# One core, sixteen batches: the last batch's final layer norm rearranged, and the planner's ranks changed

## The chip, the core and the metric

The kernel runs on one core of a Trainium2 chip. The metric is the device time of one execution in microseconds (us). Engines are named as in the profile: PE is TensorE's matmul, PEld its weight load, DVE is VectorE, ACT ScalarE, POOL GpSimd, SP SyncE, which here only issues DMA transfers (SPq in the profile).

## The reference, cut to what matters

The input x has 16 batches of 1024 nodes by 128 features; adj is a symmetric 1024x1024 matrix of zeros and ones. Two layers follow each other, each with a residual and a layer norm without weights:

```python
x = _layernorm(x + gnn_0(x, adj, ...), axis=-1)      # graph attention
x = _layernorm(x + gnn_1(x, adj, adj, ..., 5), axis=-1)  # gated, 5 steps
```

Layer 0 computes attention over pairs of nodes, masked by adj, as one product of adj with scaled features. Layer 1 repeats this step five times for every batch, with h of 1024x128 as state (in_matrix and out_matrix are both adj, and the biases are zero):

```python
m = einsum('nm,bmd->bnd', adj, h)          # messages; av = [m, m]
u3 = h @ u3_w.T + u3_b
z = sigmoid(av @ w3_w.T + w3_b + u3)
r = sigmoid(av @ w4_w.T + w4_b + u3)
hv = tanh(av @ w5_w.T + w5_b + (r * h @ u5_w.T + u5_b))
h = (1.0 - z) * h + z * hv
```

and ends, for every batch, with `layernorm(y + h)`, where y is what layer 0 gave (the "layer input" below). All values are fp32.

## The kernel before, in words

State is held transposed: hT of a batch is 128 features by 1024 nodes, worked in two halves of 512 columns, e = 0 and 1. Batches go in pairs q (batches 2q and 2q+1). For most pairs the messages of both batches are made together, with seven products in place of eight (sums of quarters, "tab"), from copies of h that are turned on VectorE and through DRAM (T, away to X, back to G). For the first pair's first three steps and the last pair's last three steps (`PLAIN`) each batch has its own messages (tiles ps_acc and blk_h).

Per batch, step and half, `gates` issues: the product with u3 (pu, L1103), ScalarE's copy of it into the bank of z (L1106), the products for r and z on top (L1113), their tanh (L1116, a sigmoid by halves), r times h on VectorE (L1123), the two products for the candidate (pv, L1129 and L1130), its tanh (hv, L1133), and three VectorE operations that make the new h: subtract (L1140), times (L1147), add (L1154).

`leave` is what follows a step. After the last one, for each half g: h is transposed back (on PE for the last three batches, L523, as `on_pe` says), the layer input is loaded again from DRAM (yd) into a tile o (L1197), VectorE adds the two (L1205), `layernorm` runs, and o goes out (L1216). `layernorm` has four parts: statistics on VectorE (four bn_stats L492, four bn_aggr L494), on GpSimd the power -1/2 of the variance and a bias from the mean (L498 to L505), and on ScalarE four operations of 128x128 that scale and shift (L510). Even batches carry the negative of h, so sign(b) is -1 for them and +1 for odd ones. The tiles o have two buffers; y0, layer 0's own result tile, has two as well and is not used once layer 0 is done.

The order in which every engine gets its instructions is not the order of the code. `Plan.add` records each operation with its engine, a length, a rank and what it reads and writes; `Plan.order` then plays the program through: an engine that is free takes, of the operations that are ready, the one with the lowest rank. Lengths on VectorE and ScalarE are taken 15% longer (`MARGIN`), and a fixed lag is added between engines. The hardware engines then run their lists strictly in that order, each waiting for what its next instruction needs. So a rank changes the order of lists and nothing else.

A step of a batch has the rank `10*(b//2) + 4.2*s`, and its operations are set off from it by the table `D` (m is the copy of messages, pu, pr, pz, pv the products, u, r, z, hv the ScalarE and VectorE work on them, h the three last operations, tr the turn or transposition, o the residual add and the load of the layer input, ln the layer norm, out the output). `LATER` is added for batch 15 in its last three steps, so that batches 14 and 15 take turns. Layer 0 and the look at adj have ranks of their own.

`IDLE` is the number of pairs of transposes of the identity that PE is given with rank 9000, that is, whenever the plan has nothing else ready for it. Each pair has a planned length of 2x109 ns. All write to one tile, ("ps", "idle"), which takes one of six "ps" banks from the first to the last of them.

Of the kernel before, what the change touches and what calls it, by code (L numbers as in the profile page):

```python
# [18 lines left out]
HALF = 512  # L19
# [6 lines left out]
LOW, HIGH = -20.0, 100.0  # L26
TINY = 1e-30
PLAIN = {(0, 0), (0, 1), (0, 2), (7, 2), (7, 3), (7, 4)}
LATER = 3
TURNED = {(7, 3)}  # L30
IDLE = 100


class Plan:
# [98 lines left out]
def kernel(  # L133
# [79 lines left out]
    def exact(pools):  # L213
# [62 lines left out]
        def chunks(ap):  # L276

            return ap.rearrange("p (b c i) -> p c b i", b=4, c=4)
# [5 lines left out]
        def pe(*a, **k):  # L284
            plan.add("PE", *a, **k)

        def dve(*a, **k):
            plan.add("DVE", *a, **k)

        def act(*a, **k):  # L290
            plan.add("ACT", *a, **k)
# [2 lines left out]
            plan.add("SP", *a, **k)  # L294


        D = dict(m=-0.4, pu=1.4, u=0.4, pr=0.8, pz=1.4, r=-0.3, pv=0.2, z=0.3, hv=0.2, h=0.6, tr=1.0, o=3.6, ln=3.9)
        D.update(out=4.2, l1=-9, l2=-5, l3=-4, l4=-4, l5=-5, l6=-3.5, l7=-1, l8=0)

        def on_pe(b, what):  # L300

            return b < 2 and what in ("y", "b") or b >= B - 3 and what == STEPS - 1 or (b // 2, what) in TURNED
# [181 lines left out]
            dve(2 * V, 1 + c / 4, t24, reads=[*y, (("tab",), c, 0)], writes=[(("tab",), c, 1)])  # L484


        def layernorm(key, g, rank, after, src, dst, write, sg=1):
            stats, mv, rstd = ("stats", *key, g), ("mv", *key, g), ("rstd", *key, g)

            def look():  # L490
                for j in range(4):
                    nc.vector.bn_stats(T(stats)[:, j, :], src(j))  # L492
                for j in range(4):
                    nc.vector.bn_aggr(T(mv)[:, j, :], T(stats)[:, j, :])  # L494

            def power():
                mean, var, r = T(mv)[:, :, 0], T(mv)[:, :, 1], T(rstd)
                nc.gpsimd.tensor_scalar(r[:, 0, :], var, EPS, None, ALU.add)  # L498
                nc.gpsimd.tensor_tensor(r[:, 0, :], r[:, 0, :], mhalf[:, 0:4], ALU.pow)
                if sg > 0:  # L500
                    nc.gpsimd.tensor_scalar(r[:, 1, :], mean, -1.0, None, ALU.mult)
                    nc.gpsimd.tensor_tensor(r[:, 1, :], r[:, 1, :], r[:, 0, :], ALU.mult)
                else:
                    nc.gpsimd.tensor_tensor(r[:, 1, :], mean, r[:, 0, :], ALU.mult)
                    nc.gpsimd.tensor_scalar(r[:, 0, :], r[:, 0, :], -1.0, None, ALU.mult)  # L505

            def scale():
                r = T(rstd)
                for j in range(4):
                    nc.scalar.activation(  # L510
                        dst(j), src(j), AF.Identity, bias=r[:, 1, j : j + 1], scale=r[:, 0, j : j + 1]
                    )

            dve(1100, rank, look, reads=[after], writes=[(stats, 0), (mv, 0)])
            plan.add("POOL", 2200, rank, power, reads=[(mv, 0)], writes=[(rstd, 0)])
            act(1250, rank, scale, reads=[after, (mv, 0), (rstd, 0)], writes=[write])

        def transposes(src, read, t, rank):


            def emit():
                for j in range(4):
                    nc.tensor.transpose(T(t)[:, j * P : (j + 1) * P], src()[:, j * P : (j + 1) * P], ident)  # L523

            pe(4 * TR, rank, emit, reads=[*read, (("ident",), 0)], writes=[(t, 0)])

        def turn(t, src, read, rank):

# [436 lines left out]
        def messages(q, s, k):  # L965
# [118 lines left out]
            combine(m[one, 1], c, ALU.add)  # L1084
            return [[(m[one, 0], 0), (m[one, 1], "part")], [(m[two, 1], "part")] * 2]

        def gates(b, s, soon):
            rank = rank_of(b, s)
            hT = ("hT", b)
            sg = sign(b)  # L1090


            for e in range(2):
                m, r, z, hv = (k + (b, s, e) for k in (("m",), ("r",), ("z",), ("hv",)))
                pr, pz, pv = ("ps", "g", b, s, e, "r"), ("gz", b, s, e), ("ps", "g", b, s, e, "v")
                mark = (("after",), b, s, e)

                def h(e=e):
                    return T(hT)[:, hs[e]]


                def pu_(pr=pr, h=h):
                    nc.tensor.matmul(T(pr), u3, h(), start=True, stop=True)  # L1103

                def u_(pr=pr, pz=pz):
                    nc.scalar.copy(T(pz), T(pr))  # L1106

                pe(F, rank + D["pu"], pu_, reads=[(hT, e), (("uw",), 0), soon[b % 2][e]], writes=[(pr, 0), mark])
                act(A, rank + D["u"], u_, reads=[(pr, 0)], writes=[(pz, 0)])
                for p_, t, j, due in ((pr, r, 1, "r"), (pz, z, 0, "z")):  # L1110

                    def gate_(p_=p_, j=j, m=m):
                        nc.tensor.matmul(T(p_), wm[:, j, :], T(m), start=False, stop=True, skip_group_check=True)  # L1113

                    def sig_(p_=p_, t=t, j=j):
                        nc.scalar.activation(T(t), T(p_), AF.Tanh, bias=bh[:, j : j + 1], scale=0.5 * sg)  # L1116

                    pe(F, rank + D["p" + due], gate_, reads=[(m, 0), mark, (pz, 0), (("wm",), 0)], writes=[(p_, 1)])
                    act(A, rank + D[due], sig_, reads=[(p_, 1)], writes=[(t, 1)])
                dve(  # L1120
                    V,
                    rank + D["r"],
                    lambda r=r, h=h: nc.vector.scalar_tensor_tensor(T(r), T(r), 1.0, h(), ALU.add, ALU.mult),  # L1123
                    reads=[(r, 1), (hT, e)],
                    writes=[(r, 2)],
                )

                def pv_(pv=pv, m=m, r=r):
                    nc.tensor.matmul(T(pv), wm[:, 2, :], T(m), start=True, stop=False)  # L1129
                    nc.tensor.matmul(T(pv), u5h, T(r), start=False, stop=True)  # L1130

                def hv_(pv=pv, hv=hv):
                    nc.scalar.activation(T(hv), T(pv), AF.Tanh, bias=b5 if sg > 0 else nb5, scale=1.0)  # L1133

                pe(2 * F, rank + D["pv"], pv_, reads=[(m, 0), (r, 2), (("wm",), 0), (("uw",), 0)], writes=[(pv, 0)])
                act(A, rank + D["hv"], hv_, reads=[(pv, 0), (("wm",), 0)], writes=[(hv, 0)])
                dve(
                    V,
                    rank + D["h"],
                    lambda hv=hv, h=h: nc.vector.tensor_tensor(T(hv), T(hv), h(), ALU.subtract),  # L1140
                    reads=[(hv, 0), (hT, e)],
                    writes=[(hv, 1)],
                )
                dve(
                    V,
                    rank + D["h"],
                    lambda hv=hv, z=z: nc.vector.scalar_tensor_tensor(T(hv), T(z), 1.0, T(hv), ALU.add, ALU.mult),  # L1147
                    reads=[(hv, 1), (z, 1)],
                    writes=[(hv, 2)],
                )  # L1150
                dve(
                    V,
                    rank + D["h"],
                    lambda hv=hv, h=h: nc.vector.scalar_tensor_tensor(h(), T(hv), 0.5, h(), ALU.mult, ALU.add),  # L1154
                    reads=[(hv, 2)],
                    writes=[(hT, e)],
                )

        def leave(b, s):

# [2 lines left out]
            for g in range(2):  # L1163
# [18 lines left out]
                    continue  # L1182

                t = ("ps", "t", b, s, g)
                if on_pe(b, s):
                    transposes(h, [(hT, g)], t, rank + D["tr"])
                else:
                    t = ("F", b, s, g)
                    turn(k, h, [(hT, g)], rank + D["tr"])
                    away(k, d, rank + D["tr"])  # L1190
                    back(d, t, rank + D["o"])

                o, yd = ("o", b, g), ("yd", b, g)
                sp(
                    450,
                    rank + D["o"],
                    lambda o=o, yd=yd: nc.sync.dma_start(T(o).rearrange("p c d -> p (c d)"), T(yd)),  # L1197
                    reads=[(yd, 0), (hT, g)],
                    writes=[(o, "y")],
                )  # L1200

                def last(t=t, o=o, flat=on_pe(b, s)):
                    x = T(o).rearrange("p c (a j) -> p c a j", a=4)
                    n = T(t).rearrange("p (c a j) -> p c a j", c=4, a=4) if flat else chunks(T(t))
                    nc.vector.tensor_tensor(x, n, x, ALU.add)  # L1205

                dve(V, rank + D["o"], last, reads=[(t, 0), (o, "y")], writes=[(o, "raw")])

                def at(j, o=o):
                    return T(o)[:, j, :]  # L1210

                layernorm(("o", b), g, rank + D["ln"], (o, "raw"), at, at, (o, 0), sign(b))
                sp(
                    450,
                    rank + D["out"],
# [343 lines left out]
```

## Time and profile before

| | us |
|---|---|
| runs of the kernel before, median of 3 (lowest, highest) | 1466.42 (1464.65, 1471.49) |
| the profiled execution: its own time | 1466.58 |
| its span, from the first to the last instruction | 1464.7 |
| PE busy / DVE busy / ACT busy / POOL busy in the span | 1442.1 / 1168.4 / 898.9 / 152.9 |
| idle transposes (L413): count, first and last start | 200, 4.9 and 49.4 |
| last product of the gates (L1130): start | 1447.99 |
| last scaling (L510): end | 1460.49 |

A row of a timeline gives the start, the length, the engine, the line and the operation with its output and inputs; "x4" means that four of them were merged into one row, and the bracket tells how long the engine was idle before it and what ended that. In a row of waits the figures are the total in us, how often, and the longest. [...] what counts for PE's rate is the distance between starts, 0.43 us for the fp32 products of the gates and 0.233 us for those with the messages' rounded type.

### The profile page before, as it was taken

How to read it: one execution, taken by the hardware profiler on the slowest of the kernel's cores; microseconds unless marked ns; L12 is line 12 of the kernel's file. 1: busy time of each engine (PE TensorE's matmuls, PEld its weight loads, DVE VectorE, ACT ScalarE, POOL GpSimd, SP SyncE). 2: the span in 40 equal slices, each digit the busy share in tenths (PEclk: the TensorE clock that was granted, in tenths of full speed). 3: DMA queues.
4: the chain of work that ended last, by engine and by line, in shares of the span. 5: the costliest groups of instructions: out<-in, count | busy, mean ns of one | idle time of the engine just before them, and what ended most of it. 6: DMA issues, size and time to landing. Idle time of an engine off the chain costs nothing.

```text
span 1464.7 us, 17943 instructions
## 1 busy us (share of the span) xinstructions
PE 1442.1 (98%) x5052; PEld 904.6 (62%) x5052; DVE 1168.4 (80%) x2757; ACT 898.9 (61%) x1792; POOL 152.9 (10%) x265
## 2 busy tenths in 40 slices
PE   9999899999999999999999999999999999999995
PEld 7766665666666666665566656665666665665563
DVE  6887788888888788888888888887888877757444
ACT  5456565676657666576756676566674666555544
POOL 0201000011002020110201120011110202000102
PEclk9999999999999999999999999999999999999998
DMA  4145534654335542464433643355433464223301
GB/s 164 58 126 162 167 78 117 172 177 128 87 100 151 173 131 65 121 172 140 117 98 117 187 123 94 108 161 155 116 85 96 134 184 114 58 72 87 91 24 45
DMA packets 208384, 174.21 MB, mean 119 GB/s; under 512 B 34879, under 2 KB 158486, under 8 KB 208278
## 3 DMA queue, kind: packets, MB, share of 16 engines
q1 hardware_dynamic: 207714, 172.15, 41.1%
q10 hardware_dynamic: 564, 0.85, 0.2%
q8 instruction: 41, 0.67, 0.2%
q14 instruction: 65, 0.53, 0.1%
HBM read 94.63 MB, written 78.29 MB: 118 GB/s over the span
## 4 chain that ended last, share of the span: by engine, by line
PE 94%; DVE 2%; DMA 1%; ACT 1%; POOL 1%; issue 0%; SPq 0%; POOLq 0%; DVEq 0%
PE ps_acc_a L573 17%; PE ps_g_r L1113 9%; PE ps_g_v L1129 9%; PE ps_g_v L1130 9%; PE gz L1113 9%; PE ps_g_r L1103 9%; PE ps_acc_c L573 8%; PE ps_acc_po L573 8%; PE ps_acc L573 6%; PE gz L573 4%; PE ps_g_ph L602 2%; PE ps_idle L413 1%; PE ps_acc_po L872 1%; PE ps_acc_px L858 1%; ACT o L510 1%; DMA blk_boot<-in_adj_dram 0%
## 5 line engine op out<-in xcount | busy, mean ns | idle before, releaser
L1129 PE MATMUL ps_g_v<-m,wm 128*128 128x512 f32 x320 | 163.4, 592 | 0.0
L1130 PE MATMUL ps_g_v<-r,u5h 128*128 128x512 f32 x320 | 163.3, 592 | 0.0
L1140 DVE TENSOR_TENSOR hv<-hv,hT 128x512 f32<-128x512 f32 x160 | 109.7, 687 | 63.2 <-ACT hv L1133 62.8
L1113 PE MATMUL ps_g_r<-m,wm 128*128 128x512 f32 x320 | 158.8, 594 | 1.1 <-ACT gz L1106 1.1
L1113 PE MATMUL gz<-m,wm 128*128 128x512 f32 x320 | 157.7, 592 | 0.0
L1103 PE MATMUL ps_g_r<-hT,u 128*128 128x512 f32 x320 | 152.7, 592 | 0.0
L1123 DVE SCALAR_TENSOR_TENSOR r<-r,hT 128x512 f32<-128x512 f32 x160 | 109.1, 686 | 50.9 <-ACT r L1116 50.1
L573 PE MATMUL ps_acc_a<-tab,blk_s 128*128 128x512 f32 x544 | 146.7, 411 | 0.4 <-ACT m L1056 0.4
L573 PE MATMUL ps_acc_po<-adj,blk 128*128 128x512 f32 x512 | 144.5, 428 | 0.0
L1116 ACT ACTIVATE r<-ps_g_r,bh 128x512 f32<-128x512 f32 x160 | 109.4, 686 | 46.8 <-PE ps_g_r L1113 46.5
L573 PEld LDWEIGHTS ps_acc_a<-tab,blk_s 128*128 128x128 f32 x544 | 100.4, 188 | 34.4 <-issue 6.7
L1116 ACT ACTIVATE z<-gz,bh 128x512 f32<-128x512 f32 x160 | 109.5, 688 | 19.1 <-PE gz L1113 18.8
L573 PEld LDWEIGHTS ps_acc_po<-adj,blk 128*128 128x128 f32 x512 | 96.0, 188 | 39.4 <-issue 14.6
L1154 DVE SCALAR_TENSOR_TENSOR hT<-hv,hT 128x512 f32<-128x512 f32 x160 | 107.9, 676 | 1.6
L1147 DVE SCALAR_TENSOR_TENSOR hv<-z,hv 128x512 f32<-128x512 f32 x160 | 108.1, 677 | 1.0 <-ACT z L1116 0.3
L1106 ACT COPY gz<-ps_g_r 128x512 f32<-128x512 f32 x160 | 91.5, 574 | 28.1 <-PE ps_g_r L1103 26.7
L531 DVE STREAM_TRANSPOSE T<-hT 128x512 f32<-128x512 f32 x150 | 104.9, 701 | 4.1 <-DMA X<-T 3.7
L1130 PEld LDWEIGHTS ps_g_v<-r,u5h 128*128 128x128 f32 x320 | 60.5, 189 | 76.8 <-issue 61.9
L1113 PEld LDWEIGHTS gz<-m,wm 128*128 128x128 f32 x320 | 60.5, 190 | 74.4 <-issue 74.0
L573 PE MATMUL ps_acc<-adj,blk_h 128*128 128x512 f32 x384 | 99.9, 416 | 3.9 <-DVE blk_h L565 3.9
L1133 ACT ACTIVATE hv<-ps_g_v,nb 128x512 f32<-128x512 f32 x80 | 54.9, 689 | 68.6 <-PE ps_g_v L1130 68.6
L1113 PEld LDWEIGHTS ps_g_r<-m,wm 128*128 128x128 f32 x320 | 59.4, 189 | 58.5 <-issue 44.6
(166 smaller groups left out, 2520.7 us busy)
## 6 DMA issues: line engine op xcount, KB each, us to landing
G<-X SPq DMA_DIRECT2D x152, 256.0 KB
X<-T SPq DMA_DIRECT2D x600, 64.0 KB
yd<-y SPq DMA_DIRECT2D x32, 256.0 KB
o<-yd SPq DMA_DIRECT2D x32, 256.0 KB
out_dram<-o SPq DMA_DIRECT2D x32, 256.0 KB
xt<-in_x_dram SPq DMA_DIRECT2D x15, 512.0 KB
pb<-ud SPq DMA_DIRECT2D x14, 512.0 KB
D_y<-T_y SPq DMA_DIRECT2D x112, 64.0 KB
```

Source lines behind the costliest of these rows:

```text
L531: nc.vector.transpose(T(t).rearrange("p (b c i) -> p b c i", b=4, c=4), turned(src()))
L573: nc.tensor.matmul(T(bank), T(blk)[:, k, c, :], right(c), start=(first and i == 0), stop=(last and i == len(terms) - 1), skip_group_check= ...
L1103: nc.tensor.matmul(T(pr), u3, h(), start=True, stop=True)
L1106: nc.scalar.copy(T(pz), T(pr))
L1113: nc.tensor.matmul(T(p_), wm[:, j, :], T(m), start=False, stop=True, skip_group_check=True)
L1116: nc.scalar.activation(T(t), T(p_), AF.Tanh, bias=bh[:, j : j + 1], scale=0.5 * sg)
L1123: lambda r=r, h=h: nc.vector.scalar_tensor_tensor(T(r), T(r), 1.0, h(), ALU.add, ALU.mult),
L1129: nc.tensor.matmul(T(pv), wm[:, 2, :], T(m), start=True, stop=False)
L1130: nc.tensor.matmul(T(pv), u5h, T(r), start=False, stop=True)
L1140: lambda hv=hv, h=h: nc.vector.tensor_tensor(T(hv), T(hv), h(), ALU.subtract),
L1147: lambda hv=hv, z=z: nc.vector.scalar_tensor_tensor(T(hv), T(z), 1.0, T(hv), ALU.add, ALU.mult),
L1154: lambda hv=hv, h=h: nc.vector.scalar_tensor_tensor(h(), T(hv), 0.5, h(), ALU.mult, ALU.add),
```

## The change

It does seven things.

1. The layer input of batch 15 is loaded into tiles of the kind y0 (keyed `("y0", b, "o", g)`), not o, and the load has the rank of the step itself, not +3.6; it waits for the first m of that step, not for h. For all batches the planned lag of this load is now 2300 ns.
2. `layernorm` gets a form `short`: GpSimd makes only the power (and its negative for even batches), and VectorE scales with four `tensor_scalar` operations, (x - mean) times r. It is used for both halves of batch 15 and for the second half of batch 14.
3. `pieces` is 2 for batch 15 in its last step: hv, the three operations on h, the transposes and the residual add are made in pieces of 256 columns.
4. `LATER` goes from 3 to 2.
5. `IDLE` goes from 100 to 140.
6. In `D`, for all batches: pz from 1.4 to 1.2, z from 0.3 to 0.5, tr from 1.0 to 1.2, out from 4.2 to 4.0.
7. Some planned lengths follow from this (a half tanh 400, a half VectorE operation V/2+40, the short scaling 900, GpSimd 1700).

```diff
-LATER = 3
+LATER = 2
-IDLE = 100
+IDLE = 140
...
-        D = dict(m=-0.4, pu=1.4, u=0.4, pr=0.8, pz=1.4, r=-0.3, pv=0.2, z=0.3, hv=0.2, h=0.6, tr=1.0, o=3.6, ln=3.9)
-        D.update(out=4.2, l1=-9, l2=-5, l3=-4, l4=-4, l5=-5, l6=-3.5, l7=-1, l8=0)
+        D = dict(m=-0.4, pu=1.4, u=0.4, pr=0.8, pz=1.2, r=-0.3, pv=0.2, z=0.5, hv=0.2, h=0.6, tr=1.2, o=3.6, ln=3.9)
+        D.update(out=4.0, l1=-9, l2=-5, l3=-4, l4=-4, l5=-5, l6=-3.5, l7=-1, l8=0)
...
-                if sg > 0:
+                if short:
+                    if sg < 0:
+                        nc.gpsimd.tensor_scalar(r[:, 0, :], r[:, 0, :], -1.0, None, ALU.mult)
+                elif sg > 0:
...
+            def scale_short():
+                for j in range(4):
+                    nc.vector.tensor_scalar(
+                        dst(j), src(j), T(mv)[:, j, 0:1], T(rstd)[:, 0, j : j + 1], ALU.subtract, ALU.mult
+                    )
+            if short:
+                dve(900, rank, scale_short, reads=[*after, (mv, 0), (rstd, 0)], writes=[write])
+            else:
+                act(1250, rank, scale, reads=[*after, (mv, 0), (rstd, 0)], writes=[write])
...
+        def pieces(b, s):
+            return 2 if b == B - 1 and s == STEPS - 1 else 1
...
+                n = pieces(b, s)
+                for i in range(n):
+                    w = slice(i * HALF // n, (i + 1) * HALF // n)
...
+                    length = V if n == 1 else V / n + 40
+                    act(A if n == 1 else 400, rank + D["hv"], hv_, reads=[(pv, 0), (("wm",), 0)], writes=[(hv, 0, i)])
+                    dve(length, rank + D["h"], less_, reads=[(hv, 0, i), (hT, e)], writes=[(hv, 1, i)])
+                    dve(length, rank + D["h"], times_, reads=[(hv, 1, i), (z, 1)], writes=[(hv, 2, i)])
+                    dve(length, rank + D["h"], h_, reads=[(hv, 2, i)], writes=[(hT, e) if n == 1 else (hT, e, i)])
...
-                o, yd = ("o", b, g), ("yd", b, g)
+                o, yd = ("y0" if b == B - 1 else "o", b, "o", g), ("yd", b, g)
                 sp(
                     450,
-                    rank + D["o"],
+                    rank + (D["o"] if b < B - 1 else 0),
                     lambda o=o, yd=yd: nc.sync.dma_start(T(o).rearrange("p c d -> p (c d)"), T(yd)),
-                    reads=[(yd, 0), (hT, g)],
+                    reads=[(yd, 0), (hT, g) if b < B - 1 else (("m", b, s, 0), 0)],
                     writes=[(o, "y")],
+                    lag=2300,
                 )
+                for i in range(n):
...
+                    dve(V / n, rank + D["o"], last, reads=[(t, i), (o, "y")], writes=[(o, "raw", i)])
...
                     sign(b),
+                    b == B - 1 or b == B - 2 and g,
                 )
```

## The prediction

> **What bounds the kernel now.** I read the page's busy shares first, then TensorE's own waits, then busy time by stretch, then the end in order of time. Page, part 1:
>
> ```profile
> PE 1442.1 (98%) x5052; PEld 904.6 (62%) x5052; DVE 1168.4 (80%) x2757; ACT 898.9 (61%) x1792; POOL 152.9 (10%) x265
> ```
>
> TensorE (PE) has work for 98% of the span. The view of waits, for PE alone, lists nearly all of its waiting:
>
> ```profile
> PE ps_acc L573 <- DVE blk_h L565: 3.9, 1, 3.9
> PE ps_t L523 <- DVE hT L1154: 2.8, 2, 2.4
> PE gz_fill L417 <- POOL ones L383: 1.3, 1, 1.3
> PE ps_g_r L1113 <- ACT gz L1106: 1.1, 2, 0.7
> PE ps_p L679 <- DVE T_ws L398: 1.0, 1, 1.0
> ```
>
> So a rank can win only three things: the one long wait (first line), small waits of under 1 us, and the end, where PE is done early. Busy time by stretch, around the long wait and at the end (columns: stretch, length, busy us of PE, weight load, VectorE, ScalarE, GpSimd, then PE's granted clock, DMA share, GB/s):
>
> ```profile
> 149.00:153.20 4.20, 0.35 (x2) 0.03 (x1) 4.17 (x7) 2.03 (x6) 0.00 (x0) 0.92 0.82 235
> 153.20:159.50 6.30, 6.27 (x15) 4.94 (x16) 2.72 (x12) 1.22 (x3) 0.00 (x0) 0.51 0.69 193
> 159.50:165.00 5.50, 5.50 (x25) 4.03 (x24) 1.57 (x3) 3.41 (x6) 0.00 (x0) 1.00 1.01 351
> ```
>
> PE stands from 149 to 153.2 while VectorE is full (4.17 of 4.20), and then runs 6.3 us at a clock of 0.51. The stall costs 3.9 us plus about 3.1 us (6.3 x 0.49) of slow clock: 7.0 us. The end, in order of time (start, length, engine, line, operation, idle before):
>
> ```profile
> 1442.06 7.48 SPq L1216 DMA_DIRECT2D out_dram<-o  x2
> ...
> 1443.16 1.13 PE L1113 MATMUL ps_g_r<-m,wm 128*128 128x512 f32 x2 [0.41 <-ACT gz L1106]
> ...
> 1446.04 0.69 ACT L1133 ACTIVATE hv<-ps_g_v,b 128x512 f32<-128x512 f32 x1 [1.03 <-PE ps_g_v L1130]
> ...
> 1447.49 1.64 ACT L510 ACTIVATE o<-o,rstd_o 128x128 f32<-128x128 f32 x4
> ...
> 1449.03 0.67 ACT L1133 ACTIVATE hv<-ps_g_v,b 128x512 f32<-128x512 f32 x1
> 1449.59 2.32 SPq L1197 DMA_DIRECT2D o<-yd  x2
> ...
> 1452.53 0.69 DVE L1205 TENSOR_TENSOR o<-ps_t,o 128x512 f32<-128x512 f32 x1 [0.59 <-DMA o<-yd]
> ...
> 1458.84 1.65 ACT L510 ACTIVATE o<-o,rstd_o 128x128 f32<-128x128 f32 x4 [0.37 <-POOL rstd_o L502]
> ```
>
> The reload of the layer input (L1197) leaves SP only at 1449.59, because the output of batch 14 (L1216) stands before it in SP's order, waiting for ScalarE's scaling to end. VectorE's first residual add (L1205) waits for that load until 1452.53. One scaling (L510 at 1447.49) stands before the last tanh (L1133, 1449.03). From the end of the last scaling (1460.49) to the end of the span are 4.2 us of output transfer.
>
> [...] 4 us of idle, then 0.51 for 6.3 us. [...] here the stretch from 22.6 to 28.5 us holds, but for eight tiny products at its end, only 50 idle transposes and keeps a clock of 1.00, so the trace decides: idle transposes keep the clock. [...]
>
> **The change, part by part: the end.** All of this lies after the last PE work and is on the path.
>
> Reload: it moves from rank +3.6 to the start of step 4 of batch 15 (trigger: the first m) and goes to y0 tiles, which layer 0 has left long ago. That m is copied at about 1433, so it lands before it is needed, and one DMA issue (0.4 us) goes ahead of batch 14's outputs on SP, which do not start before 1442.06: free. What is late next is VectorE itself.
>
> Pieces: the last step of batch 15 has 8 chain instructions (2 tanh, 6 VectorE) and 2 residual adds, which become 16 and 4. At full size VectorE starts one every 0.605 us (L475/L476 rows near 53 us); [...] The six halves of an e take 2.04 us against 1.81: more work, but the first starts after a tanh of 0.47 instead of 0.69.
>
> Scaling: four 128x128 operations on VectorE instead of four of 480 ns on ScalarE (1.65 us in all). The nearest row is L433, a 128x128 tensor_scalar of 216 ns; with the spacing of the bn_stats (four in 0.87 us) as the upper end, 0.6 to 0.87; I take 0.66. GpSimd's two last operations (0.24 + 0.20 us, 0.6 with their gaps) go for batch 15. For the second half of batch 14 the scaling leaves ScalarE, and with it what stood before the last tanh; its 0.66 us is now on VectorE, behind batch 15's lower ranks.
>
> LATER 3 to 2: batch 15 moves one rank forward. Its u3 products of step 3 have rank 84.6+1.4 = 86.0, now below batch 14's messages of step 4 (86.8); before it was 87.0. So the two batches' gates are done in turn instead of mixed, and batch 14's first scaling (L510 at 1440.38, which held up the gz copy) comes earlier. A batch alone in its gates costs no wait in the trace: from 1388.28 to 1396.58 batch 14 alone does its 20 matmuls of 0.43 us (8.6) without a gap. I count the 0.57 us lost before 1443.16 as gone.
>
> The sum: first tanh 1446.04-0.57 = 1445.47; +0.47+0.05: VectorE starts at 1445.99; six halves: 1448.03. The last product starts 0.57 earlier, 1447.42, and its tanh 0.63 later as for the first e (1445.41 to 1446.04), 1448.05; +0.52: 1448.57; six halves: 1450.61; four half adds (1.36): 1451.97; two sets of statistics at 1.15 (1453.25 to 1454.40): 1454.27; to GpSimd 0.45 and its two operations 1.35: 1456.07; scaling 0.1+0.66: 1456.83; output 4.2: 1461.0. Against 1464.7 that is 3.7 us. If the 0.57 stays and batch 14's scaling comes between, it is 2.5; if the first e's adds and statistics fit in VectorE's gaps, up to 5.
>
> **The rest of the program.** D's new ranks hold for all batches: z products before u3 products, z's tanh after the u copy, the turn of h (and so its away and back transfers on SP) after the combining of messages, outputs earlier on SP. Behind a later turn stand its four DMA issues (1.8 us on SP) and the fetch of G; ScalarE already waits 31.7 us for G without PE standing. Since PE has no wait of note between 165 and 1440, nothing is to be gained there beyond about 1 us; the loss is bounded by one more stall of the size above, 7.0. I take 0.
>
> IDLE 100 to 140 adds 80 transposes at 0.109 us: 8.7 us of PE work. In the trace the 100 pairs are used up at 49.5, so the new ones go to later places where the planner sees PE idle. Laid into the long wait they cost nothing and keep the clock: -3.1. Laid where PE is really full they cost 0.218 a pair, +8.7 at most. The wait takes 18 pairs; that leaves 22, part of which will fall in the planner's gaps between 50 and 149 that the trace does not show as waits. I take 14 of them uncovered (+3.1) against the clock (-3.1): 0, with both ends kept.
>
> Forecast: 3.7 us less. The profiled execution took 1466.58 with 1464.7 of span (1.9 around it); the median is 1466.42, so the step is the same there: **1462.7 us**.
>
> **Rivals.**
> First, the long wait itself goes: VectorE's queue there (six h operations, two turns, then blk_h) is ordered anew, or idle work keeps the clock and some of the wait falls away. For it: it hangs on the order of one queue. Against: blk_h has rank 8.4 and all that stands ahead (4.8 to 8.0) stays ahead under the new ranks. 1462.7-7.0 to 1462.7-3.1: about 1457.
> Second, slower: the idle pairs are uncovered. The planner counts VectorE and ScalarE 15% long, so it sees gaps on PE that are none; each pair there pushes all later work. It decides from 17 pairs on (3.7/0.218). All 40: 1462.7+8.7 = 1471.4.
> Third: the shared idle tile keeps one of six ps banks until its last use, 49.5 us before and perhaps far later now, or a later turn makes PE wait for messages: one or two stalls of 7.0, 1469.7 to 1476.7.
>
> **How the numbers follow.** Forecast 0.43, first rival 0.22, second 0.18, third 0.17. What can be told from no change is about 0.5%, 7.3 us: under 1459.1 and over 1473.7. The first rival lies nearly whole under it, with a little of the forecast's spread: 0.23; the third by more than half, the second partly: 0.19; 0.58 between. The likeliest case alone reaches from 1460 to 1466; for 8 in 10 the range goes from 1456 to 1474.
>
> **What would show it.** In the changed profile: o<-yd issued before batch 14's outputs; no wait of L1205 for a DMA; L1133 and the three h lines at 128x256 near 340 ns apart; PE's last product near 1447.4 plus what came before; from there 13.6 us to the end instead of 16.7. The idle tile's last use and PE's clock after 149 us show which idle case holds. I am wrong if PE shows a new wait of over 2 us in the middle, or idle matmuls between products that had no gap before.

## The result and the profile after

| | before | after |
|---|---|---|
| median of the runs (lowest, highest), us | 1468.95 (1464.65, 1471.49), 7 runs | 1479.81 (1476.23, 1482.15), 7 runs |
| ratio after/before, 95% interval | | 1.0079 (1.0064 to 1.0093) |
| span of the profiled execution | 1464.7 | 1479.9 |
| start of the last product of the gates | 1447.99 | 1465.05 |
| from there to the end of the span | 16.71 | 14.82 |

The kernel became 0.8% slower. 1462.7 had been forecast with a range to 1474, so the result lies outside on the slow side. In the later series of runs the kernel before took 1465.35 to 1466.73 us (medians), not 1468.95; against 1466 the kernel after would stand at 1.0094, and that is the value to set beside the ratios of the experiments. The last two rows divide it: the end, which nearly the whole prediction was about, became 1.9 us shorter. All that comes before it, which the prediction put at nothing, became 17.1 us longer.

In what follows lines are numbered as in the kernel after. L1120, L1123, L1130, L1133, L1140, L1147 and L1155 are the gates' L1103, L1106, L1113, L1116, L1123, L1130 and L1133 of before; L586 is L573 (messages), L574 and L578 are L561 and L565 (a block for the messages is cut into two parts), L513 is L510 (scaling on ScalarE), L519 the new scaling on VectorE. Kernels made from the one before keep its numbers.

Busy time on the page of the kernel after:

```profile
PE 1452.9 (98%) x5132; PEld 912.3 (62%) x5132; DVE 1169.6 (79%) x2777; ACT 892.8 (60%) x1782; POOL 147.2 (10%) x260
```

PE still has work for 98% of the span. It is busy for 10.8 us more, and 8.7 of these are the 80 new idle transposes at 0.109 us. What PE waited for (total us, how often, longest):

```profile
PE ps_g_r L1130 <- ACT gz L1123: 6.3, 5, 2.1
PE ps_t L536 <- DVE hT L1164: 2.4, 1, 2.4
PE ps_acc L586 <- DVE blk_h L578: 2.3, 3, 1.6
PE ps_g_v L1147 <- DVE r L1140: 1.8, 1, 1.8
PE gz_fill L417 <- POOL ones L383: 1.3, 1, 1.3
```

Where one wait of 3.9 us headed this list before, five waits for ScalarE's copy gz do now. Busy time by stretch around the old long wait, same columns as before:

```profile
149.00:153.20 4.20, 3.72 (x15) 2.42 (x14) 3.07 (x7) 2.44 (x6) 2.64 (x4) 1.00 0.20 53
153.20:159.50 6.30, 6.30 (x31) 4.61 (x30) 6.09 (x15) 4.70 (x12) 0.00 (x0) 1.00 0.74 237
```

All but 0.48 us of the long wait is gone, and PE's clock stays at 1.00. So 6.5 of the 7.0 us were won there, and the loss elsewhere must be more than 17. The idle transposes did not do it. One tile's instructions, the idle tile's (shortest, median and longest ns, first and last start):

```profile
L413 PE MATMUL ps_idle<-ident x280: 271/273/476, 4.9 to 1388.0; 128*128 128x128 f32 x140
```

All but 66 are used up by 51 us; these stand in twelve small groups between products from 194 to 1388 us, 18 of them at 829.5, and none in the old long wait.

What the new waits look like shows at the longest one. The timeline of the kernel after, columns as before:

```profile
877.63 2.74 PE L1120 MATMUL ps_g_r<-hT,u 128*128 128x512 f32 x6
...
878.20 3.59 POOL L507 TENSOR_TENSOR rstd_o<-mv_o,rstd_o 128x4 f32<-128x4 f32 x1
...
881.87 0.24 POOL L508 TENSOR_SCALAR rstd_o<-rstd_o 128x4 f32<-128x4 f32 x1
882.15 1.65 ACT L513 ACTIVATE o_o<-o_o,rstd_o 128x128 f32<-128x128 f32 x4 [3.63 <-POOL rstd_o L508]
...
883.70 1.05 ACT L1123 COPY gz<-ps_g_r 128x512 f32<-128x512 f32 x2
...
884.33 3.55 PE L1130 MATMUL ps_g_r<-m,wm 128*128 128x512 f32 x4 [2.10 <-ACT gz L1123]
```

From the bottom up: PE stood 2.10 us for gz (ScalarE's copy of the u3 product). ScalarE could have copied it as soon as the u3 product was there (L1120, from 877.63), but its list has a layer norm's scaling first (L513), and that stood 3.63 us for GpSimd, whose operation L507 took 3.59 us. The plan counts 2200 ns for all of GpSimd's part; here it took over 5. The scaling has no hurry; but ScalarE's list is run in order, and the copies behind the scaling start at 883.70, as it ends, and are late with it.

The wait costs PE more than its length. Busy time by stretch just behind it:

```profile
884.60:888.00 3.40, 3.40 (x5) 1.36 (x5) 0.69 (x1) 1.48 (x4) 0.20 (x2) 0.50 0.49 119
```

For 3.4 us the clock is at 0.50, which is 1.7 us more. In the kernel before, half clock came with the wait of 3.9 us (0.50 from 152.5 to 159.3 us); here it came behind one of 2.10 us. What makes it come isn't shown: behind the wait of 2.37 us that ends at 1451.99 us in the kernel before, PE's four transposes (0.66 us) still ran at 1.00.

The wait at 860.8 us (1.80, the page's "DVE r") is of the same kind on VectorE. The chain of waits of the kernel after (start, length, what):

```profile
853.85 4.41 DMA F<-X
...
858.29 0.70 DVE o_o L1231
...
861.95 0.61 DVE r L1140
...
862.60 1.13 PE ps_g_v L1147 x2
```

A residual add (L1231) waits for a fetch of 4.41 us that is planned at 2.3, and r, for which PE waits, comes behind it on VectorE.

Last, the end:

```profile
1464.62 1.02 PE L1147 MATMUL ps_g_v<-r,u5h 128*128 128x512 f32 x2
...
1465.66 1.11 DVE L519 TENSOR_SCALAR o_o<-o_o,mv_o,rstd_o 128x128 f32<-128x128 f32 x4
1465.68 0.84 ACT L1155 ACTIVATE hv<-ps_g_v,b 128x256 f32<-128x256 f32 x2 [1.03 <-PE ps_g_v L1147]
1466.68 0.76 DVE L1158 TENSOR_TENSOR hv<-hv,hT 128x256 f32<-128x256 f32 x2
...
1468.60 1.09 PE L536 MATMUL ps_t<-ident,hT 128*128 128x128 f32 x4 [2.36 <-DVE hT L1164]
...
1469.72 0.76 DVE L1231 TENSOR_TENSOR y_o<-ps_t,y_o 128x256 f32<-128x256 f32 x2 [0.27 <-PE ps_t L536]
...
1474.42 1.12 DVE L519 TENSOR_SCALAR y_o<-y_o,mv_o,rstd_o 128x128 f32<-128x128 f32 x4 [0.22 <-POOL rstd_o L499]
```

No residual add of batch 15 waits for a DMA any more, and the pieces are there. But the scaling of batch 14's second half (L519, 1.11 us) stands on VectorE right where the last pieces could start.

### The profile page after: what moved, and what is told of

It is laid out like the page before. It is cut to its first block, busy times and chain, and to the rows that moved or that the text cites. A ratio compares the mean times of both kernels' runs of the same rounds, so it can differ in the third digit from the quotient of the medians.

```text
span 1479.9 us, 18030 instructions
## 1 busy us (share of the span) xinstructions
PE 1452.9 (98%) x5132; PEld 912.3 (62%) x5132; DVE 1169.6 (79%) x2777; ACT 892.8 (60%) x1782; POOL 147.2 (10%) x260
## 4 chain that ended last, share of the span: by engine, by line
PE 86%; DMA 4%; DVE 3%; SPq 2%; ACT 2%; issue 1%; POOL 1%; DVEq 0%; POOLq 0%; ACTq 0%
PE ps_acc_a L586 15%; PE ps_g_r L1130 8%; PE ps_g_v L1147 8%; PE ps_g_v L1146 8%; PE ps_g_r L1120 8%; PE gz L1130 8%; PE ps_acc_po L586 8%; PE ps_acc_c L586 8%; PE ps_acc L586 5%; PE gz L586 4%; DMA G<-X 2%; SPq L554 2%; PE ps_idle L413 2%; PE ps_g_ph L615 2%; PE ps_acc_po L885 1%
## 5 line engine op out<-in xcount | busy, mean ns | idle before, releaser
L1130 PE MATMUL ps_g_r<-m,wm 128*128 128x512 f32 x320 | 161.0, 601 | 7.5 <-ACT gz L1123 6.3
L1147 PE MATMUL ps_g_v<-r,u5h 128*128 128x512 f32 x320 | 163.4, 592 | 1.8 <-DVE r L1140 1.8
L1158 DVE TENSOR_TENSOR hv<-hv,hT 128x512 f32<-128x512 f32 (+1 forms) x162 | 110.2, 682 | 65.4 <-ACT hv L1155 65.2
L1130 PE MATMUL gz<-m,wm 128*128 128x512 f32 x320 | 158.5, 593 | 0.0
L1140 DVE SCALAR_TENSOR_TENSOR r<-r,hT 128x512 f32<-128x512 f32 x160 | 109.6, 689 | 60.1 <-ACT r L1133 59.3
L1120 PE MATMUL ps_g_r<-hT,u 128*128 128x512 f32 x320 | 153.8, 592 | 0.0
L586 PE MATMUL ps_acc_a<-tab,blk_s 128*128 128x512 f32 x544 | 148.4, 414 | 0.8 <-ACT m L1069 0.8
L586 PE MATMUL ps_acc_po<-adj,blk 128*128 128x512 f32 x512 | 142.8, 425 | 0.0
L1133 ACT ACTIVATE r<-ps_g_r,bh 128x512 f32<-128x512 f32 x160 | 109.5, 686 | 53.1 <-PE ps_g_r L1130 52.8
L586 PEld LDWEIGHTS ps_acc_a<-tab,blk_s 128*128 128x128 f32 x544 | 100.8, 188 | 33.5 <-issue 9.6
L586 PEld LDWEIGHTS ps_acc_po<-adj,blk 128*128 128x128 f32 x512 | 96.0, 188 | 37.9 <-issue 12.5
L1133 ACT ACTIVATE z<-gz,bh 128x512 f32<-128x512 f32 x160 | 109.7, 688 | 14.9 <-PE gz L1130 14.3
L1123 ACT COPY gz<-ps_g_r 128x512 f32<-128x512 f32 x160 | 91.3, 572 | 37.6 <-PE ps_g_r L1120 36.3
L1164 DVE SCALAR_TENSOR_TENSOR hT<-hv,hT 128x512 f32<-128x512 f32 (+1 forms) x162 | 108.6, 673 | 1.2
L1147 PEld LDWEIGHTS ps_g_v<-r,u5h 128*128 128x128 f32 x320 | 60.4, 189 | 79.0 <-issue 62.6
L1161 DVE SCALAR_TENSOR_TENSOR hv<-z,hv 128x512 f32<-128x512 f32 (+1 forms) x162 | 108.4, 671 | 0.8 <-ACT z L1133 0.2
L1130 PEld LDWEIGHTS gz<-m,wm 128*128 128x128 f32 x320 | 60.6, 191 | 74.6 <-issue 74.3
L586 PE MATMUL ps_acc<-adj,blk_h 128*128 128x512 f32 x384 | 101.6, 414 | 2.3 <-DVE blk_h L578 2.3
L1130 PEld LDWEIGHTS ps_g_r<-m,wm 128*128 128x128 f32 x320 | 59.3, 190 | 63.3 <-issue 39.3
L1155 ACT ACTIVATE hv<-ps_g_v,nb 128x512 f32<-128x512 f32 x80 | 54.9, 688 | 68.8 <-PE ps_g_v L1147 68.5
```

What stands on the lines that cost most here:

```text
L586: nc.tensor.matmul(T(bank), T(blk)[:, k, c, :], right(c), start=(first and i == 0), stop=(last and i == len(terms) - 1), skip_group_check= ...
L1158: nc.vector.tensor_tensor(T(hv)[:, w], T(hv)[:, w], h()[:, w], ALU.subtract)
L1161: nc.vector.scalar_tensor_tensor(T(hv)[:, w], T(z)[:, w], 1.0, T(hv)[:, w], ALU.add, ALU.mult)
L1164: nc.vector.scalar_tensor_tensor(h()[:, w], T(hv)[:, w], 0.5, h()[:, w], ALU.mult, ALU.add)
```

## The experiments

After the result four theories were open for the 17 us ahead of the end. R, the redrawn order: every edit to a rank, a planned length or a lag lets the planner draw all lists anew, and the order before happens to fit the chip well, so that any other has more waits. A, the bank: the idle tile holds one of the six banks that PE's results go to, until 1388 us (the prediction's third rival). I, the time of the idle transposes (its second rival). D, the new ranks are worse as such. A fifth, P, came from the rows above: the plan's times for fetches and GpSimd are too short. For each kernel I give the ratio to the kernel before with its 95% interval, and mostly the start of the last product, which was 1447.99 before and 1465.05 after.

**Idle work and the bank.** The kernel after with 100 pairs, and the kernel before with 140:

```diff
-IDLE = 140
+IDLE = 100
```

```diff
-IDLE = 100
+IDLE = 140
```

> The changed kernel with IDLE back at 100; all else as changed. Theory A (the bank: the idle tile, now last written at 1388 us, keeps one of six ps banks nearly to the end, and the planner, short of a bank, leaves PE short waits): both the 8.7 us of idle transposes and most of the 15 us of new short waits between 150 and 1390 us go; ratio to before 0.995 to 1.000. Theory B (the new ranks make the waits): only the 8.7 us go; ratio near 1.002 and the waits of PE for gz (L1123) stay, some 6 us.

> The kernel before with IDLE at 140 and nothing else. Here 64 of the 80 added transposes come around the long wait at 149 us and the last at its end, so the bank is free again early. Theory A: the clock stays up through the wait, ratio 0.997 to 1.000. Theory C (added idle transposes cost their time wherever they stand): 8.7 us more, ratio 1.006.

Measured: 1.0118 (1.0101 to 1.0135) and 1.0170 (1.0153 to 1.0187). Without its 8.7 us of idle work the kernel after is slower still (last product at 1467.9), and the long wait of 4.0 us at 149 is back. The kernel before with more idle work puts 64 transposes into and around its long wait, which goes as hoped, and loses 26 us: 8.7 of idle work, the rest by new waits elsewhere of up to 4.0 us (at 903 us; another of 1.9 at 1398). Theory I isn't decided by this. Taking the transposes out doesn't give their time back, but it draws another order too: PE's list leaves that of the kernel after at 68 us.

The bank was tried by itself: each added pair gets its own tile, so that none is held between them; and, the other way round, the kernel after with 100 pairs plus one late pair that holds the bank.

```diff
-                nc.tensor.transpose(T(("ps", "idle"))[:, j * P : (j + 1) * P], ident, ident)
+                nc.tensor.transpose(T(("ps", "idle", i))[:, j * P : (j + 1) * P], ident, ident)
```

```diff
+        pe(2 * TR, rank_of(14, 3), idle_, reads=[(("m", 14, 3, 0), 0), (("ident",), 0)], writes=[(("ps", "idle"), 0)])
```

> The changed kernel with IDLE at 140, where each of the 40 added pairs writes a tile of its own that is given back at once; the first 100 share one as before. The time of 80 transposes stays, the bank is free from 50 us. Theory A: ratio 0.997 to 1.003, well under the changed kernel's 1.008. Theory C (it is the transposes' time) or B: as the changed kernel, 1.006 to 1.009.

> The changed kernel with IDLE at 100 and one more idle pair that waits for a message of batch 14's step 3, so that the idle tile keeps its bank until about 1370 us; only 0.2 us of PE work more than with IDLE at 100. Theory A: 8 to 15 us over the run with IDLE at 100, ratio 1.003 to 1.007. Theory B or C: as the run with IDLE at 100.

Measured: own tiles 1.0208 (1.0191 to 1.0225); bank held 1.0122 (1.0105 to 1.0139). That it was held, the idle tile's row of this kernel shows:

```profile
L413 PE MATMUL ps_idle<-ident x202: 270/273/332, 4.7 to 1412.0; 128*128 128x128 f32 x101
```

Held to 1412 us the bank shows no cost: 1.0122 against 1.0118 for its twin that frees it at 49 us; and freed between the added pairs it wins nothing. Both are new orders as well (PE's list leaves the twin's at 70 us, the kernel after's at 71), so that a small cost isn't excluded. But nothing speaks for theory A.

**The end alone.** The edits to the end on the kernel before, with IDLE 100, LATER 3 and the old ranks; then the same with LATER 2. The first against the kernel after, and the second against the first:

```diff
-LATER = 2
-IDLE = 140
+LATER = 3
+IDLE = 100
...
-pz=1.2, r=-0.3, pv=0.2, z=0.5, hv=0.2, h=0.6, tr=1.2, o=3.6, ln=3.9)
-        D.update(out=4.0,
+pz=1.4, r=-0.3, pv=0.2, z=0.3, hv=0.2, h=0.6, tr=1.0, o=3.6, ln=3.9)
+        D.update(out=4.2,
...
-                    lag=2300,
+                    lag=2300 if b == B - 1 else None,
```

```diff
-LATER = 3
+LATER = 2
```

> The kernel before with only the edits of batch 15's end and the short layer norm (reload into y0, scaling on VectorE, pieces of 256 columns); ranks, LATER and IDLE as before, the planned lag of 2300 ns for batch 15's load alone. PE's list is then row for row that of before. Theory R (the loss comes from a new order of the lists, not from an edit): 1.9 to 3.7 us faster, ratio 0.9975 to 0.9987. Theory T (the end's edits cost elsewhere): slower than before.

> As the run before it, with LATER at 2. PE's list is that of before up to row 1257 of 2808 in difference only where batches 14 and 15 are concerned (similarity 0.993). Theory R: ratio 0.996 to 1.001, since little is redrawn. Theory L (LATER 2 itself costs, as the 1.8 us waits near 1390 us in the changed kernel suggest): 1.001 to 1.003.

Measured: 0.9984 (0.9977 to 0.9991) and 0.9974 (0.9964 to 0.9984). PE's list is the old one in the first of the two, and its last product starts at 1448.03, as before; from there to the end it takes 14.75 us, and 14.31 in the second. What PE waited for in the second:

```profile
PE ps_acc L586 <- DVE blk_h L578: 4.0, 1, 4.0
PE ps_t L536 <- DVE hT L1164: 2.4, 1, 2.4
PE gz_fill L417 <- POOL ones L383: 1.3, 1, 1.3
PE ps_g_r L1130 <- ACT gz L1123: 0.7, 1, 0.7
```

The long wait is there as before; the wait ahead of 1443.16 is gone. PE's list is that of before up to 1403.9 us, and yet PE is 1.4 us ahead there. That isn't the edit's doing. Busy time in the stretch behind the long wait of this kernel:

```profile
153.20:159.50 6.30, 6.11 (x20) 4.84 (x21) 2.85 (x13) 1.64 (x4) 0.00 (x0) 0.73 0.65 161
```

The half clock behind the same wait lasts 3.4 us here and 6.8 us in the kernel before (0.73 against 0.51 in this stretch). To LATER 2 belong the 0.6 us that PE gains from 1403.9 us to its last product, and the 0.4 us at the end. So the end's edits give what they can give where the order ahead of them stays. Over all kernels of this study those with the end's edits need 14.3 to 14.9 us from the last product on, and those without 16.6 to 16.8.

**Redrawing alone.** If R holds, an edit that means nothing must cost as much. VectorE's planned length of 605 ns was set to 606, 604 and 607 in the kernel before; nothing that runs on the chip changes but the order:

```diff
-        R, F, TR, V, A = 233, 858, 109, 605, 640
+        R, F, TR, V, A = 233, 858, 109, 606, 640
```

> The kernel before with the planned length of one VectorE operation at 606 in place of 605 ns. No operation, rank or count is changed, only the planner's arithmetic; PE's list differs from row 250 on (similarity 0.847, the changed kernel's is 0.855). Theory R: slower than before by 5 to 30 us, ratio 1.004 to 1.020, with new waits of PE in other places. Theory D (the new ranks are at fault): no change, 0.998 to 1.002.

> The kernel before with the planned VectorE length at 604 ns: a second neutral redraw. Theory R: 1.004 to 1.020. Theory D (only what the diff sets is bad): 0.998 to 1.002.

> The kernel before with the planned VectorE length at 607 ns: a third neutral redraw. Theory R: 1.004 to 1.020. Theory D: 0.998 to 1.002.

Two parts of the change were tried by themselves as well: the planned lag of the layer input's load, and the new ranks D:

```diff
+                    lag=2300,
```

```diff
-pz=1.4, r=-0.3, pv=0.2, z=0.3, hv=0.2, h=0.6, tr=1.0, o=3.6, ln=3.9)
-        D.update(out=4.2,
+pz=1.2, r=-0.3, pv=0.2, z=0.5, hv=0.2, h=0.6, tr=1.2, o=3.6, ln=3.9)
+        D.update(out=4.0,
```

> The kernel before with one edit of the diff that changes no operation: the planned lag of the layer input's load, 2300 in place of 2500 ns, for all batches. PE's list differs from row 543 on. Theory R: ratio 1.004 to 1.020. Theory D: 0.998 to 1.002.

> The kernel before with the new table D and nothing else. Theory R: it lies among the neutral redraws, 1.004 to 1.020. Theory D: it lies above them, and carries most of the changed kernel's 11 us by itself.

| kernel | ratio (95%) | last product, us |
|---|---|---|
| length 606 | 1.0132 (1.0117 to 1.0148) | 1464.79 |
| length 604 | 1.0147 (1.0126 to 1.0167) | 1469.24 |
| length 607 | 1.0076 (1.0054 to 1.0098) | 1461.53 |
| planned lag of the load | 1.0048 (1.0032 to 1.0063) | 1457.96 |
| new ranks D alone | 1.0144 (1.0124 to 1.0164) | 1469.83 |

One nanosecond in a planned length costs 1.3%, more than the whole change. The kernel with 606, what PE waited for:

```profile
PE ps_g_r L1113 <- ACT gz L1106: 5.6, 5, 2.5
PE ps_acc L573 <- DVE blk_h L565: 4.4, 2, 4.2
PE ps_t L523 <- DVE hT L1154: 2.8, 2, 2.4
PE ps_acc_a L573 <- ACT m L1058: 2.7, 1, 2.7
PE gz L573 <- ACT gz L1056: 2.7, 1, 2.7
```

Waits for gz stand first here too, and its timeline has the same picture as the one at 882 us: GpSimd's last operation ends late, the scaling waits, the copy stands behind it.

```profile
1386.92 0.48 POOL L502 TENSOR_TENSOR rstd_o<-rstd_o 128x4 f32<-128x4 f32 x1
1387.44 1.65 ACT L510 ACTIVATE o<-o,rstd_o 128x128 f32<-128x128 f32 x4 [2.77 <-POOL rstd_o L502]
1388.99 0.56 ACT L1029 COPY m<-ps_acc 128x512 f32<-128x512 f32 x1
1389.46 1.05 ACT L1106 COPY gz<-ps_g_r 128x512 f32<-128x512 f32 x2
1390.09 1.13 PE L1113 MATMUL ps_g_r<-m,wm 128*128 128x512 f32 x2 [2.47 <-ACT gz L1106]
```

R holds: a new order alone costs as much as the change. The traces show it directly, too. In these five kernels PE's list is that of before, product for product, up to 289 us (606), 247 (604), 196 (607), 610 (lag) and 403 (ranks), and there PE is between 0.9 us ahead and 2.4 us behind; the rest of the 10.0 to 21.8 us by which their last products are late comes after the lists part. Theory D has nothing left to explain: the ranks alone cost 1.4%, within what the meaningless edits cost.

**Mending one kind of wait by hand.** The kernel after, with each output scaling on ScalarE put up to three places later in ScalarE's list, and the three lists of PE, VectorE and GpSimd left exactly as they were. `later` moves every scaling of a tile o behind up to three of ScalarE's following operations:

```diff
-            for i in plan.order():
+            for i in later(plan.order(), 3):
```

> The changed kernel with each output scaling (L513) put up to three places later in ScalarE's list, with its output transfer behind it; PE's, VectorE's and GpSimd's lists are row for row the changed kernel's. In the changed kernel's trace two waits of PE, 2.1 us at 882 and 1.9 at 1389, end with a gz copy that stood behind such a scaling, which itself waited for GpSimd. Theory H (late items at the head of an in-order list hold PE): these two go, 2 to 5 us less than the changed kernel, ratio 1.0045 to 1.007. Theory N (the waits only move to the next instruction): as the changed kernel, 1.0075 to 1.0095.

Measured: 1.0097 (1.0080 to 1.0114), no gain over 1.0079. What PE waited for:

```profile
PE ps_g_r L1133 <- ACT gz L1126: 3.4, 4, 1.6
PE ps_t L539 <- DVE hT L1167: 2.4, 1, 2.4
PE ps_acc L589 <- DVE blk_h L581: 2.0, 3, 1.4
PE ps_acc_a L589 <- ACT m L1072: 1.9, 1, 1.9
PE ps_acc_a L589 <- ACT m L1074: 1.6, 1, 1.6
```

The waits for gz fall from 6.3 to 3.4 us. At 882 us the whole wait goes, and PE, 2.6 us behind the kernel after at 880 us, is 1.4 ahead at 890: 4.0 us, about the 2.1 of the wait and the 1.7 of half clock behind it. So the late scaling was the cause there. Of the 3.5 us of new waits for m, the 1.9 at 371 us are the move's own, since a scaling that was put off (370.82 to 372.46) now stands just ahead of that copy. The 1.6 at 237 us are not: ScalarE's list differs from 334 us on only, and this wait ends with a fetch of G that came later in this execution. What the move wins at one place it loses at another.

**Longer planned times.** If P is the general cause, a plan that counts 3500 ns for a fetch (2300 before) and for GpSimd's part of a layer norm (2200 before) should suffer less from being drawn anew. First as twins of the three meaningless edits:

```diff
-            plan.add("POOL", 2200, rank, power, reads=[(mv, 0)], writes=[(rstd, 0)])
+            plan.add("POOL", 3500, rank, power, reads=[(mv, 0)], writes=[(rstd, 0)])
...
-                lag=2300,
+                lag=3500,
```

> The kernel before planned with VectorE at 604 ns, and with longer planned times for what was late in the traces: 3.5 us for a fetch from DRAM (2.3 before) and 3.5 us for GpSimd's part of a layer norm (2.2 before). No operation is changed. Theory P (redraws lose because the plan's times for transfers and GpSimd are too short): well under its twin with the old lengths (1.0147), 1.000 to 1.006. Theory Q (the order before is one good draw among many, and better times in the plan don't change that): 1.004 to 1.020 again.

> The same longer planned times with VectorE at 606 ns; its twin with the old ones was at 1.0132. Theory P: 1.000 to 1.006. Theory Q: 1.004 to 1.020.

> The same longer planned times with VectorE at 607 ns; its twin with the old ones was at 1.0076. Theory P: 1.000 to 1.006. Theory Q: 1.004 to 1.020.

Then on the kernel after itself, and on it with 100 idle pairs:

> The changed kernel itself, planned with 3500 ns in place of 2300 for the fetch of the turned h and 3500 in place of 2200 for GpSimd's part of a layer norm; nothing else is changed. Theory P (the planned times are shorter than what these two take, so that operations which wait for them stand too early in the lists): as in the three twins on the kernel before, most of the loss goes: 0.996 to 1.003 of the kernel before, PE's waits for gz and m under 3 us together. Rival R alone (any redrawn order has its own chance waits, and the longer times are one more redraw): anything from 1.004 to 1.015, waits of 5 us and more at new places.

> The same with IDLE 100 in place of 140. Its twin with the short planned times gave 1.0118. Theory P: 0.995 to 1.002 (as the run beside it, less up to 8.7 us of transposes, plus up to 7 us if the long wait near 149 us comes back). Rival R alone: 1.004 to 1.015.

| kernel | short planned times | long planned times (95%) |
|---|---|---|
| before, length 604 | 1.0147 | 1.0047 (1.0029 to 1.0066) |
| before, length 606 | 1.0132 | 0.9994 (0.9985 to 1.0003) |
| before, length 607 | 1.0076 | 1.0017 (1.0007 to 1.0027) |
| after | 1.0079 | 1.0195 (1.0178 to 1.0212) |
| after, IDLE 100 | 1.0118 | 1.0100 (1.0083 to 1.0117) |

All three twins improve, which speaks for P; the last two rows speak against it. On the kernel whose loss was to be explained it made things worse. What PE waited for there first:

```profile
PE ps_acc L586 <- ACT blk_h L574: 6.5, 1, 6.5
PE ps_t_u L654 <- ACT u L639: 4.8, 2, 3.3
PE ps_acc_a L586 <- ACT m L1069: 3.9, 6, 0.9
PE ps_g_r L1130 <- ACT gz L1123: 2.9, 4, 0.9
```

The waits for gz did fall, from 6.3 to 2.9 us. Two new ones follow each other at 158 and 162 us (3.3 and 6.5 us, the latter behind a fetch of G for which ScalarE stands 6.26 us); together they outweigh that, and PE's clock is at 0.50 from 160.6 to 177.7 us, 8.5 us more:

```profile
160.60:177.70 17.10, 9.42 (x21) 6.42 (x22) 7.43 (x25) 5.00 (x9) 0.00 (x0) 0.50 0.76 215
```

So a late fetch or a late GpSimd is the cause of a wait at the places shown, but as the general cause of the loss P isn't shown: the three twins may have been lucky draws. One of them (606, 0.9994) is as good as the kernel before, so R's "any other" goes too far: most new orders were worse here, not all. What makes the order before so good stays open.

**The long wait, filled by hand.** Since t2 (the end's edits with LATER 2) keeps the long wait and its slow clock, 16 pairs of transposes were put directly ahead of the waiting product, into its own bank, which the product then begins anew. No list changes otherwise:

```diff
+WARM = 16
...
+                    if bank == ("ps", "acc", 0, 2, 0) and first:
+                        for i in range(2 * WARM):
+                            j = i % 2
+                            nc.tensor.transpose(T(bank)[:, j * P : (j + 1) * P], ident, ident)
+                    product(bank, blk, right, first, last, seeded=not (first or plain(q, s)))
```

> The run with the end's edits and LATER at 2, with 16 pairs of idle transposes (3.5 us) put into PE's list just ahead of the product that PE waits for at 149 us; they write into that product's own bank, which it then overwrites, so no bank is held and no other list changes. The prediction's claim on idle work in the long wait: PE's clock stays at 1.00 after it and the end comes 2.5 to 3.5 us earlier, ratio to before 0.994 to 0.9965. If idle transposes don't keep the clock, or delay the product: 0.997 to 1.000.

Measured: 0.9970 (0.9958 to 0.9982), against 0.9974 without them. Busy time by stretch in this kernel:

```profile
149.00:153.20 4.20, 4.20 (x38) 3.91 (x36) 4.17 (x8) 2.41 (x8) 0.00 (x0) 1.00 0.81 240
153.20:159.50 6.30, 5.75 (x26) 4.65 (x26) 3.23 (x13) 1.81 (x4) 0.00 (x0) 1.00 0.71 213
```

and a little later:

```profile
175.88 0.68 DVE L1148 SCALAR_TENSOR_TENSOR r<-r,hT 128x512 f32<-128x512 f32 x1
...
176.62 1.12 PE L1155 MATMUL ps_g_v<-r,u5h 128*128 128x512 f32 x2 [0.96 <-DVE r L1148]
```

The clock stays at 1.00 (0.73 in the second stretch without them), and the block of products that waited ends at 161.10 in place of 162.26. By 165 us the lead is down to 0.35 us, as the next block of products comes no earlier for VectorE, and at 175.7 PE waits 0.96 us for r, a wait that the kernel without them doesn't have: VectorE, 4.17 of 4.20 us busy in the first stretch, is what sets the pace here. The last product starts at 1445.86 against 1445.93.

These two kernels, with LATER 2 and with the 16 pairs (medians 1462.03 and 1462.08 us), beat both the kernel before and the one after. That the first comes so near to the forecast of 1462.7 is in part luck: its end takes 14.3 us and not 13.6, and 1.4 us of what it has won in the trace is the shorter half clock.

## Why the prediction was wrong

**The rest of the program: this step failed.** "I take 0", with a loss "bounded by one more stall of the size above, 7.0". The last product starts 17.1 us later, although the long wait was gone. For 8.7 of this PE is busy with the idle transposes, and 8.3 is the net of all waits and slow clock; with the 6.5 won at 149 us added back, the new waits cost about 15. The eight of them over 0.7 us make 11.2, and the half clock behind the longest 1.7; the rest is smaller waits that I have not assigned one by one. The reasoning was local: each changed rank was asked for what stands next to it, and PE's few waits were taken as a sign of slack. They were the sign of an order that fits, and the bound of one stall has no base, since each redrawn list has its own waits: five edits to the kernel before that touch no more than a planned length, a lag or the ranks cost 0.5 to 1.5%. Both signs that the prediction had named for its being wrong came: a new wait of over 2 us in the middle (2.10 at 882 us), and idle transposes between products.

**IDLE at 0.** Wrong in its picture: no pair fell into the long wait. In the kernel after they stand between products, most of them far from it, 8.7 us in all. Not all of it is lost: of the largest group, 1.96 us from 829.50, the first 1.1 pass before the gz copy that the next product needs has ended (830.57). What the pairs cost by themselves stays open, because another number of pairs is another order.

**The end, 3.7 us with the 0.57.** The mechanism was right and its size was off: from the last product's start to the end 13.6 us were forecast, 14.8 were measured, 14.3 with LATER 2 on the old ranks. The forecast's 0.34 us from one half operation on VectorE to the next and its 0.47 for a half tanh were the author's estimates; measured were 0.35 (six in 2.10) and 0.471 (L1155, 128x256, mean of four). By terms, in the kernel after: the first of the last pieces started 1.00 us after the start of its tanh, not 0.52, because batch 14's scaling, which the sum had behind it, stood before it on VectorE (+0.48); six halves took 2.10 and not 2.04 (+0.06); the four half adds 1.70, not 1.36, since PE's last transposes took 1.09 us (0.66 in the kernel before), at a clock of 0.50 after PE had stood 2.36 us, and held up an add by 0.27 (+0.34); both sets of statistics were 0.2 faster (-0.21); GpSimd as forecast (+0.02); the last scaling 1.15 with its gap, not 0.76 (+0.39); the output 4.33, not the 4.17 that the sum left for it (+0.16). The sum is 1.24. The largest term is the scaling, 0.87 us in two places. It was sized from L433, 216 ns, a multiplication by an immediate (a constant in the instruction); 345 ns were measured. The trace of before had a nearer row: L812, also 128x128, takes one value per partition as its scalar as L519 does, and takes 343 ns, though it reads a second tensor as well. L433 is 1.6 times as fast as L519. Whether the per-partition operands are the reason isn't shown: L519 also does two operations instead of one, and writes over its input.

**The 0.57 us before 1443.16** went with LATER 2, and only with it: the wait of 0.41 is still in the kernel with LATER 3. The gates of the two batches are done in turn, as forecast: in the kernel after the last tanh of batch 15's step 3 starts at 1437.37 us and batch 14's first u3 product of step 4 at 1439.47, with no wait at the end of it; in the kernel before such a product of batch 14 stood among those of batch 15 (L1103, from 1412.79). But batch 14's first scaling does not come earlier. It comes behind both gz copies (1460.77, they start at 1457.45 and 1458.36), and so holds up neither.

**The reload** was right: no add of batch 15 waits for it.

**The rivals.** The first one's event came (the long wait went) and was no gain in the sum; the second gave the right size of the idle work, but not its removal's effect; the third had stalls in the middle on the slow side, but as its cause a held bank, of which no cost was found, and one or two stalls where there were eight.

## What to carry to other kernels

Where a planner draws the order of in-order lists, a change to any of its numbers is first of all a new draw: before a rank or a length is judged, price the draw itself with edits that mean nothing (here 0.8 to 1.5% for one or two nanoseconds), and keep the good order fixed for edits that touch only one end. A bottleneck engine that is 98% busy with almost no waits has little to win from new ranks and much to lose. And a wait can have a second price: behind one of 2.1 us PE ran at half clock for 3.4 us. Take an operation's price from the row with the same kind of operands, not only the same operation and size: here the one said 343 ns, the other 216, and 345 were measured.

## What was not expected of the hardware

GpSimd's operations on 128x4 values vary widely. One tile's row of the kernel after (shortest, median, longest ns):

```profile
L507 POOL TENSOR_TENSOR rstd_o<-mv_o,rstd_o x15: 200/287/3587, 329.1 to 1459.8; 128x4 f32<-128x4 f32 x15
```

The longest is the one at 878.20. Through its 3.6 us VectorE runs without a gap, mostly operations with two tensor inputs. The others of this kernel go the same way: of GpSimd's operations in the layer norms other than the power, the 57 during which VectorE ran no operation with two tensor inputs took at most 0.25 us, and the two that took over 1 us (3.59 and 1.07) had such operations beside them nearly throughout. That these are the cause isn't shown: no run here took VectorE's work away.

Idle transposes kept PE's clock up where they filled a wait, as the prediction had read it from the stretch from 22.6 to 28.5 us: behind the long wait 0.73 became 1.00 in the kernel with 16 pairs. And PE's clock alone was worth little there, 0.07 us at the last product, since another engine set the pace (VectorE, 4.17 of 4.20 us busy).
